# Gathers, combines, spline rows and a norm spread over more attention heads; other order of loads, stores and gating around the experts

## The chip, the cores and the metric

One core of one Trainium2 chip runs the whole kernel: TensorE (PE) for matmuls and transposes, VectorE (DVE), ScalarE (ACT), GpSimd (POOL) and SyncE (SP), which here issues DMAs only. The metric is the device time of one execution in microseconds (us), as the median of several runs. All data are 32-bit floats except where a bf16 or int32 tile is named.

## The reference, cut to what matters

Two transformer layers over `x` of 4 batches x 512 tokens x 256 features. Each layer is "modulated": six vectors per batch, worked out from a small input `c`, scale, shift and gate the branches.

```python
# layer 0
mod = (silu(L0_c) @ L0_wmod).reshape(4, 6, 1, 256)         # sa, ca, ga, sb, cb, gb
ga, gb = sign(ga) * max(|ga|, 0.25), sign(gb) * max(|gb|, 0.25)
h = layernorm(x) * (1 + ca) + sa
q, k, v = split(h @ W + b)                                  # norms and sum over the tokens
x = x + ga * (q / |q|) * sum(k / |k| * v)
h = layernorm(x) * (1 + cb) + sb
x = x + gb * moe(h)
# moe: 2048 tokens, 32 experts, 6 chosen per token, at most 48 tokens an expert (first come)
#   yb[e] = (silu(g) * u) @ w_down[e],  g, u = split(xb[e] @ w_gate_up[e])   # [48,256]x[256,352], [48,176]x[176,256]
#   out[t] = sum over the token's experts of 16 * prob * yb[slot]            # dropped where the expert is full
#   out   += (silu(gs) * us) @ ws_down,  gs, us = split(h @ ws_gate_up)      # the shared expert
# layer 1, with its own mod
h = layernorm(x) * (1 + ca) + sa
q, k, v = h @ w_q + b_q, h @ w_k + b_k, h @ w_v + b_v       # 16 heads of 128
x = x + ga * (softmax(causal(q @ k.T / sqrt(128))) @ v @ w_o + b_o)
h = layernorm(x) * (1 + cb) + sb
gate_w, up_w, down_w = three cubic splines over control points  # 1024 x 256 each
x = x + gb * ((silu(h @ gate_w.T) * (h @ up_w.T)) @ down_w.T)
```

## The kernel before

The work is written out in one Python function. A scheduler orders the instructions of DVE, ACT, POOL and SP by program order and by what it thinks will be ready; PE's order from the experts on is the one written (`manual_schedule`). `tc.issue_after(i)` keeps what stands inside it from being issued ahead of instruction `i`. Every engine works through its own list in order, so a waiting instruction holds all that stand behind it on its engine.

**Front, 0 to about 150 us.** Layer 0's attention and the routing of its experts, batch by batch. `choose` and `place` (L542, L615) find each token's experts and places; `place` makes four one-hot tiles `oh` per batch on DVE (L649), which PE reads (L654). The routed rows go to a table in HBM. SP loads the weights of the first `NEARLY` = 5 expert pairs while there is room (L472).

**Experts, about 150 to 240 us.** 32 experts in 16 pairs. `NLOAD` = 8 slots hold the weights of eight pairs, `wg` (704 KB) and `wd` (352 KB): pair q+8 is loaded when pair q has left its slot (`load_experts`, L454, called at L870). For each pair PE does `gate_up(q+1)`, `act_turned(q)`, `turned(q+2)` and `down(q-1)`, with a piece of the shared expert (`shared_down`) and of layer 1's modulation between them. `down(q)` ends in `ysb`, a tile with two buffers: ACT writes it from PSUM (L839); POOL scatters its rows for batch 0 into `planes` in HBM (L855; the last four pairs go by a one-hot matmul instead, `combined`); an ACT-queue DMA stores all of it into `ytab` in HBM (L868), from where batches 1 to 3 are gathered later. Hence `ysb(q+2)` can be written only when the store and the scatter of `ysb(q)` have landed. The PSUM tile `py` of `down` has one buffer, so `down(q+1)` needs `ysb(q)` written.

At q = 8, SP issues the loads of the biases `bia` (three of 8 KB) and `bo`, then of layer 1's first attention weights w_q, w_k, w_v (L957 to L963). ACT scales each w_q (`scale_q`, L758). At q = 12, `read_back` (L905) reads `planes` back as four tiles `yr`, after all scatters. `gated(i)` (L920) sums the six rows of a token, adds the shared expert `ysum[0]` (L928), multiplies by the gate (L929) and adds to `x` (L930); it runs on POOL for i = 0 and on DVE for i = 1 to 3. Then come the last pieces of the shared expert, copied from PSUM by ACT (L726), and layer 1's first norm.

**Attention of layer 1, about 246 to 996 us.** 64 heads (4 batches x 16), one loop step n each (L1504), of about 11.6 us. The projections (`project`, `values`) and the output product (`out_step`) are done by a seven-product scheme, for which POOL makes sums and differences of the weights (`weight_forms`, `out_weights`, `out_forms`); PE reads these early and late in a step. Beside it, in program order, run: `gather` (L278) of batches 1 to 3, six rounds r of four tiles i each, added into `ysum[b]` by DMAs that POOL prepares; `combine(b)` (L290), which gates the sum and adds it to `x` on DVE, all four tiles in the step with n mod 16 = 10; `norm(b)`, with its statistics (`ln_stats`, L186), one step later; `spline(u)` (L1118), 24 units of six DVE instructions and two PE transposes; `ffn_forms` on POOL; and at n = 59 in program order `ffn_norm(0)`, which is bound to no instruction.

**FFN of layer 1, about 996 to 1172 us.** Not touched.

DMAs issued by SP go into one hardware queue (q1 in the profile), those issued by ACT into another (q10), POOL's indirect ones into a third (q0). The scheduler gives SP's and ACT's DMAs eight semaphores in turn, so a DMA waits until the one eight before it, of either engine, has landed.

Of the kernel before, what the change touches and what calls it, by code (L numbers as in the profile page):

```python
# [34 lines left out]
NEARLY = 5  # L35
# [45 lines left out]
def kernel(ctx: ExitStack, tc: tile.TileContext, a: dict, out: bass.AP):  # L81
# [99 lines left out]
    last_pow = [None]  # L181
# [4 lines left out]
    def ln_stats(b, name, after):  # L186

        st = small.tile([P, NTT, 6], F32, tag="st", name=f"st_{name}{b}")
        ag = small.tile([P, NTT, 2], F32, tag="ag", name=f"ag_{name}{b}")
        with after_or_not(after):  # L190
            for i in range(NTT):
                nc.vector.bn_stats(st[:, i, :], xs[b][:, i, :])
                nc.vector.bn_aggr(ag[:, i, :], st[:, i, :])
        rs = small.tile([P, NTT], F32, tag="rs", name=f"rs_{name}{b}")
        nc.vector.tensor_scalar_add(rs, ag[:, :, 1], EPS)
        last_pow[0] = nc.gpsimd.tensor_tensor(rs, rs, nhalf, ALU.pow)
        return ag, rs
# [80 lines left out]
    def gather(b, r, after):  # L278

        for i in range(NTT):  # L280
            ga = nc.gpsimd.indirect_dma_start(  # L281
                out=ysum[b][:, i, :],
                out_offset=None,
                in_=ytab[:, :],
                in_offset=bass.IndirectOffsetOnAxis(ap=code[:, b * NTT + i, r : r + 1], axis=0),
                compute_op=ALU.add,
            )
            wait_for(ga, [after])

    def combine(b, after):  # L290

        for i in range(NTT):
            y, xi = ysum[b][:, i, :], xs[b][:, i, :]
            with tc.issue_after(after.ins):
                nc.vector.tensor_tensor(y, y, gbr[:, b, :], ALU.mult)
                nc.vector.tensor_tensor(xi, xi, y, ALU.add)
# [5 lines left out]
    with ExitStack() as l0:  # L302
# [312 lines left out]
        def place(b):  # L615
# [32 lines left out]
            for i in range(NTT):  # L648
                oh = rp.tile([P, CAP, E], BF16, tag="oh", name=f"oh{b}{i}", bufs=3)  # L649
                nc.vector.tensor_tensor(  # L650
                    oh, posb[:, i : i + 1, :].to_broadcast([P, CAP, E]), iota_c, ALU.is_equal
                )
                for q in range(4):
                    nc.tensor.matmul(  # L654
                        pix[32 * q : 32 * q + 32, :, :],
                        lhsT=tok[:, b * NTT + i, :],
                        rhs=oh[:, :, 8 * q : 8 * q + 8],
                        start=(i == 0),
                        stop=(i == NTT - 1),
                    )  # L660
# [54 lines left out]
        def shared_down(i):  # L715

            pd = psa.tile([P, D], F32, tag=f"su{i % 2 if i < NEXP or i >= NI - 4 else 0}", name=f"pd{i}", bufs=1)
            for c, n in enumerate(SHC):
                nc.tensor.matmul(
                    pd,  # L720
                    lhsT=sT[0:n, c, i * P : (i + 1) * P],
                    rhs=wsd[0:n, c, :],
                    start=(c == 0),
                    stop=(c == 2),
                )
            nc.scalar.copy(ysum[i // NTT][:, i % NTT, :], pd)  # L726
# [46 lines left out]
        ewp.append(ew.enter_context(tc.tile_pool(name="ew2", bufs=1)))  # L773
        for q in range(NEARLY, NLOAD):
            loaded.append(load_experts(q))
        with tc.tile_pool(name="eps", bufs=2, space=PSUM) as ps:
# [43 lines left out]
            def down(q):  # L820
# [47 lines left out]
                nc.scalar.dma_start(out=ytab[1 + q * P : 1 + (q + 1) * P, :], in_=ysb)  # L868
                if q + NLOAD < NPAIR:
                    loaded.append(load_experts(q + NLOAD))  # L870
                if q + 8 < NPAIR:
                    fetched(q + 8)
# [47 lines left out]
            def gated(i, after):  # L920

                eng = nc.vector if i else nc.gpsimd
                yr, xi, h3 = back[i], xs[0][:, i, :], 3 * D
                with tc.issue_after(after.ins):
                    eng.tensor_tensor(yr[:, 0:h3], yr[:, 0:h3], yr[:, h3:], ALU.add)
                    for w in (1, 2):
                        eng.tensor_tensor(yr[:, 0:D], yr[:, 0:D], yr[:, w * D : (w + 1) * D], ALU.add)
                    eng.tensor_tensor(yr[:, 0:D], yr[:, 0:D], ysum[0][:, i, :], ALU.add)  # L928
                    eng.tensor_tensor(yr[:, 0:D], yr[:, 0:D], gbr[:, 0, :], ALU.mult)  # L929
                    eng.tensor_tensor(xi, xi, yr[:, 0:D], ALU.add)  # L930

            w1, s1 = load_mod_inputs(m1p, 1, nc.scalar)
            with tc.manual_schedule(engines={mybir.EngineType.PE}):
# [8 lines left out]
                for q in range(NPAIR + 1):  # L942
# [12 lines left out]
                    if q == NPAIR - NLOAD:  # L955
                        with tc.issue_after(last_load[0].ins):
                            for j, n in enumerate(("b_q", "b_k", "b_v")):  # L957
                                nc.sync.dma_start(out=bia[:, j, :], in_=a[n])
                            nc.sync.dma_start(out=bo, in_=a["b_o"])
                            load_qk(0)  # L960
                            load_v(0)
                            for n in (1, 2):
                                load_qk(n)  # L963
                    if q == NPAIR - NDIR:
                        read_back()
                    if q in (3, 5, 7):
# [18 lines left out]
                for i in range(NI - 4, NI):  # L985
                    shared_down(i)
# [5 lines left out]
        for j in range(3):  # L992
            nc.sync.dma_start(out=win[:, j, :, :], in_=a["windows"][j].rearrange("(r p) k -> p r k", p=P))
# [112 lines left out]
    with ExitStack() as att1:  # L1106
# [11 lines left out]
        def spline(u):  # L1118
            r, j = divmod(u, 3)
            t, c = basis[r], win[:, j, r, :]  # L1120
            w = sp.tile([P, D], F32, tag="spw", name=f"spw{u}")
            nc.vector.tensor_scalar_mul(w, t[:, 1, :], c[:, 1:2])
            for q in (2, 3, 4):
                nc.vector.scalar_tensor_tensor(w, t[:, q, :], c[:, q : q + 1], w, ALU.mult, ALU.add)  # L1124
# [27 lines left out]
        def norm(b):  # L1152
            hT = new_hT(hp, b, "a1")
            ln_transposed(np_, ps, "pj", 1, b, SA, CA, hT, "a1")
# [6 lines left out]
        def weight_forms(key, w, early):  # L1161
# [4 lines left out]
            if early:  # L1166
# [3 lines left out]
                nc.gpsimd.tensor_tensor(w2, A22, w3, ALU.subtract)  # L1170
                wc[key] = {2: w2, 3: w3}
            else:
# [324 lines left out]
        gathers = {r + 1: (1, r) for r in range(TOPK)}  # L1497
        for b in range(2, B):
            for r, n in enumerate((-4, -3, 2, 3, 4, 5)):
                gathers[(b - 1) * NH + n] = (b, r)  # L1500
# [3 lines left out]
        for n in range(NHD + 1):  # L1504
# [13 lines left out]
            project(n + 1, 2)  # L1518
            out_step(n, 1) if n >= LAG else free()
# [9 lines left out]
            with tc.issue_after(last_form[0].ins):  # L1529
                out_prepare(n)  # L1530
            load_qk(n + 4)
            if n == 1:
                load_v(2)
            elif n % 4 == 0 and n:
                load_v(n // 4 + 2)
            if n % 2 == 0 and 6 <= n and unit < 3 * NCH:
                with tc.issue_after(evicted[n].ins):
                    spline(unit)
                if unit in (1, 4, 7):
                    ffn_forms(unit // 3, early[:, unit // 3])  # L1540
# [18 lines left out]
            if n in gathers:  # L1559
                gather(*gathers[n], evicted[n])  # L1560
            if n // NH + 1 < B:
                if n % NH == 10:
                    combine(n // NH + 1, evicted[n])
# [3 lines left out]
            if n == NHD - 5:  # L1567
                ffn_norm(0)
# [229 lines left out]
```

## Time and profile before

| | |
|---|---|
| median of 3 runs | 1174.84 us (1174.59 to 1176.95) |
| the profiled execution | 1174.33 us |
| its span, first to last instruction | 1172.6 us |
| mean granted TensorE clock | 0.988 |
| PE busy | 1121.6 us, 96% |
| DVE / POOL / ACT busy | 860.2 / 621.2 / 536.3 us |
| HBM traffic | 73 GB/s over the span; 268 to 304 GB/s from 152 to 205 us |

An instruction in a timeline is given with its start, its duration, its engine and line, what it writes and reads, and in brackets how long its engine had stood idle before it and what ended the wait. `PEclk` is the clock that PE was granted. Line numbers are those of the kernel before.

### The profile page before, as it was taken

Reading aid. Unit: us, or ns where it says so; the run is one execution under the profiler, and the core shown is the slowest. Engines: PE = TensorE matmul, PEld = TensorE weight load, DVE = VectorE, ACT = ScalarE, POOL = GpSimd, SP = SyncE. Lnnn points to the kernel's source line nnn. Section 1 sums busy time; section 2 is a strip of 40 time slices with the busy share of each in tenths; the row PEclk is TensorE's granted clock in tenths of the full one; section 3 lists DMA queues with packets and bytes.
Section 4 is the critical chain, followed back from the end, with each engine's and each line's share of the span. In section 5 each row is a group of like instructions: output and inputs, shape, how many; then the busy total and the mean of one; then the engine's idle time right before and its main releaser. Section 6 shows DMA issues by size and latency. Waiting matters only on the chain.

```text
span 1172.6 us, 16886 instructions
## 1 busy us (share of the span) xinstructions
PE 1121.6 (96%) x5220; PEld 823.0 (70%) x5220; DVE 860.2 (73%) x2596; ACT 536.3 (46%) x1373; POOL 621.2 (53%) x945
## 2 busy tenths in 40 slices
PE   6888999879999999999999999999999999999998
PEld 2434354457777777777778777777777777888887
DVE  5688623467888788788887888888877677467765
ACT  3542223335555545554555555554555455333321
POOL 3354124328974856965565975444535655344331
PEclk9999899889999999999999999999999999999999
DMA  7801289734421312321221431011010000000001
GB/s 268 285 26 43 83 250 284 227 113 84 88 64 41 76 43 66 75 68 36 66 57 46 94 64 59 26 39 60 28 37 28 19 18 1 1 1 19 18 1 37
DMA packets 80486, 86.10 MB, mean 73 GB/s; under 512 B 12158, under 2 KB 64748, under 8 KB 80268
## 3 DMA queue, kind: packets, MB, share of 16 engines
q1 hardware_dynamic: 65564, 68.10, 18.6%
q0 software_dynamic: 11712, 13.25, 6.8%
q10 hardware_dynamic: 3120, 3.68, 1.0%
q8 instruction: 42, 0.69, 0.2%
q14 instruction: 48, 0.39, 0.1%
HBM read 73.84 MB, written 11.55 MB: 73 GB/s over the span
## 4 chain that ended last, share of the span: by engine, by line
PE 61%; DVE 9%; POOL 3%; ACT 3%; issue 1%; DMA 1%; SPq 0%; ACTq 0%; DVEq 0%; POOLq 0%
PE s L1293 10%; PE o L1334 9%; PE po L1029 7%; PE P0p L1029 6%; PE fP L1029 6%; PE pt L1325 5%; PE P1p L1029 4%; PE P2p L1029 3%; PE acc L1029 3%; PE P0v L1029 3%; PE P2v L1029 2%; PE P1v L1029 2%; POOL ysum L281 1%; DVE spw L1124 1%; DVE nm L1305 1%
## 5 line engine op out<-in xcount | busy, mean ns | idle before, releaser
L1308 ACT ACTIVATE p<-s,nm 128x512 f32<-128x512 f32 (+3 forms) x256 | 135.4, 529 | 117.1 <-DVE nm L1305 115.0
L1293 PE MATMUL s<-qk,qk 128*128 128x512 f32 (+3 forms) x512 | 170.2, 435 | 1.3 <-DVE qk L1201 1.0
L1334 PE MATMUL o<-pT,v 128*128 128x512 f32 (+3 forms) x512 | 148.6, 433 | 0.2 <-DVE u3v L1213 0.2
L1334 PEld LDWEIGHTS o<-pT,v 128*128 128x128 f32 x512 | 96.8, 190 | 55.0 <-issue 30.6
L1327 ACT COPY pT<-pt 128x512 f32<-128x512 f32 (+1 forms) x192 | 98.4, 513 | 68.2 <-PE pt L1325 66.4
L1305 DVE TENSOR_REDUCE nm<-s 128x1 f32<-128x512 f32 (+3 forms) x256 | 124.1, 485 | 4.0
L281 POOL DMA_INDIRECT ysum<-ytab,code x72 | 113.0, 1570 | 20.4 <-issue 15.5
L1310 DVE TENSOR_SCALAR p<-p,den 128x512 f32<-128x512 f32 (+3 forms) x256 | 117.6, 460 | 3.4
L1325 PEld LDWEIGHTS pt<-ident,p 128*128 128x128 f32 x640 | 81.7, 141 | 34.4 <-issue 10.5
L1325 PE MATMUL pt<-ident,p 128*128 128x128 f32 x640 | 101.7, 273 | 0.3 <-DVE p L1310 0.3
L1303 DVE TENSOR_TENSOR s<-s,mask 128x128 f32<-128x128 f32 x256 | 73.5, 287 | 31.2 <-PE s L1293 31.2
L1168 POOL TENSOR_TENSOR w_p<-w_q,w_k 128x128 f32<-128x128 f32 x63 | 38.7, 615 | 87.2 <-ACT t1p L1207 53.0
L1293 PEld LDWEIGHTS s<-qk,qk 128*128 128x128 f32 x512 | 77.5, 191 | 5.9 <-issue 1.5
L1029 PE MATMUL P0p<-hT_a,w_q 128*128 128x256 f32 x252 | 75.0, 379 | 0.0
L1176 POOL TENSOR_TENSOR w_p<-w_k 128x128 f32<-128x128 f32 x63 | 29.9, 475 | 81.0 <-PE P2p L1029 81.0
L1029 PEld LDWEIGHTS P0p<-hT_a,w_q 128*128 128x128 f32 x252 | 47.5, 190 | 33.1 <-issue 29.9
L1309 DVE RECIPROCAL den<-den 128x1 f32<-128x1 f32 x256 | 40.4, 158 | 38.4 <-ACT p L1308 33.6
L1029 PE MATMUL P1p<-fT,w_p 128*128 128x256 f32 x252 | 64.9, 380 | 2.4 <-POOL w_p L1170 1.2
L1345 ACT ACTIVATE oH<-o,bia 128x512 f32<-128x512 f32 x64 | 44.0, 687 | 42.1 <-PE o L1334 41.1
L1201 DVE SCALAR_TENSOR_TENSOR qk<-P0p,bia,u3p 128x256 f32<-128x256 f32 x63 | 30.4, 482 | 37.1 <-ACT qk L1222 36.1
L1037 POOL TENSOR_TENSOR fI<-it 128x256 f32<-128x256 f32 x30 | 21.8, 728 | 67.0 <-DVE it L1623 67.0
L1029 PEld LDWEIGHTS P1p<-fT,w_p 128*128 128x128 f32 x252 | 47.6, 190 | 9.9 <-issue 1.9
(338 smaller groups left out, 2683.2 us busy)
## 6 DMA issues: line engine op xcount, KB each, us to landing
wg<-in_w_gate_up SPq DMA_DIRECT2D x16, 704.0 KB
w_q<-in_w_q SPq DMA_DIRECT2D x64, 128.0 KB
w_k<-in_w_k SPq DMA_DIRECT2D x64, 128.0 KB
w_v<-in_w_v SPq DMA_DIRECT2D x16, 512.0 KB
wd<-in_w_down SPq DMA_DIRECT2D x16, 352.0 KB
basis<-in_basis SPq DMA_DIRECT2D x8, 640.0 KB
planes<-zero SPq DMA_DIRECT2D x4, 768.0 KB
yr<-planes SPq DMA_DIRECT2D x4, 768.0 KB
```

The lines of the kernel that those rows point to most:

```text
L281: ga = nc.gpsimd.indirect_dma_start(out=ysum[b][:, i, :], out_offset=None, in_=ytab[:, :], in_offset=bass.IndirectOffsetOnAxis(ap=code[:, ...
L1029: nc.tensor.matmul(out, lhsT=lhsT, rhs=rhs, start=start, stop=stop, skip_group_check=shared)
L1293: nc.tensor.matmul(s[:, at[i] : c], lhsT=qk[n, 0][:, i * P : (i + 1) * P], rhs=qk[n, 1][:, : (i + 1) * P], start=True, stop=True,)
L1303: nc.vector.tensor_tensor(s[:, e - P : e], s[:, e - P : e], mask, ALU.add)
L1305: nc.vector.tensor_reduce(nm, s[:, e - w : e], AX.X, ALU.max, negate=True)
L1308: nc.scalar.activation(p, s[:, e - w : e], AF.Exp, bias=nm, accum_out=den)
L1309: nc.vector.reciprocal(den, den)
L1310: nc.vector.tensor_scalar_mul(p, p, den)
L1325: nc.tensor.transpose(pt[:, c : c + P], probs[n, i][:, j * P : (j + 1) * P], ident)
L1327: nc.scalar.copy(pT, pt[:, :w])
L1334: nc.tensor.matmul(o[:, j * P :], lhsT=vs[n // 4][:, j, hc : hc + HD], rhs=pTs[n, j], start=(j == 0), stop=(j == NTT - 1),)
L1345: nc.scalar.activation(oT, o, AF.Identity, bias=bia[:, 2, h : h + 1])
```

## The change

The parts of the diff, in the order of the code:

- `NEARLY` 5 to 6: one pair more is loaded in the front, one less beside the experts; to make room, `oh` has two buffers instead of three.
- The loads of `bia` and `bo` stand ahead of the loads of pairs 6 and 7, and no longer at q = 8.
- The store of `ysb` into `ytab` is issued by SP, after the load of pair q+8, and no longer by ACT.
- `gated` no longer adds `ysum[0]`; a new `shared_gated(i)` gates it and adds it to `x` on DVE at q = 4 to 7.
- ACT's part of layer 1's first norm is issued after the last copy of the shared expert.
- `gather` handles one tile of one round at a time; 24 of them per batch are spread over 9 steps (batch 1, from n = 0) or 12 steps (from n = 12 and n = 28), up to three a step, six for one tile i before the next tile begins. The old form waited for `evicted[n]`; the new one is ordered by `issue_after` behind a weight form.
- `combine` handles one tile in each of four steps, and takes that tile's norm statistics with it; `ln_stats` uses them.
- `spline` is cut in two: three DVE instructions at odd n, three and the transposes at even n. `ffn_forms` of the first three chunks moves to n = 10, 26 and 42.
- `ffn_norm(0)` is bound to `evicted[59]`.
- The small `windows` loads stand in step 0 of the loop instead of ahead of the attention.

```diff
-NEARLY = 5
+NEARLY = 6
...
+        if b in stats:
+            _, ag = stats.pop(b)
+        else:
...
-    def gather(b, r, after):
-        for i in range(NTT):
-            ga = nc.gpsimd.indirect_dma_start(
...
-            wait_for(ga, [after])
-    def combine(b, after):
-        for i in range(NTT):
+    def gather(b, i, r):
+        nc.gpsimd.indirect_dma_start(
...
+    def combine(b, i, after):
...
+            nc.vector.tensor_tensor(xi, xi, y, ALU.add)
+            nc.vector.bn_stats(st[:, i, :], xi)
+            nc.vector.bn_aggr(ag[:, i, :], st[:, i, :])
...
-                oh = rp.tile([P, CAP, E], BF16, tag="oh", name=f"oh{b}{i}", bufs=3)
+                oh = rp.tile([P, CAP, E], BF16, tag="oh", name=f"oh{b}{i}", bufs=2)
...
+        for j, n in enumerate(("b_q", "b_k", "b_v")):
+            nc.sync.dma_start(out=bia[:, j, :], in_=a[n])
+        nc.sync.dma_start(out=bo, in_=a["b_o"])
         for q in range(NEARLY, NLOAD):
             loaded.append(load_experts(q))
...
-                nc.scalar.dma_start(out=ytab[1 + q * P : 1 + (q + 1) * P, :], in_=ysb)
                 if q + NLOAD < NPAIR:
                     loaded.append(load_experts(q + NLOAD))
+                nc.sync.dma_start(out=ytab[1 + q * P : 1 + (q + 1) * P, :], in_=ysb)
...
-                    eng.tensor_tensor(yr[:, 0:D], yr[:, 0:D], ysum[0][:, i, :], ALU.add)
...
+            def shared_gated(i, after):
+                y, xi = ysum[0][:, i, :], xs[0][:, i, :]
+                with tc.issue_after(after.ins):
+                    nc.vector.tensor_tensor(y, y, gbr[:, 0, :], ALU.mult)
+                    nc.vector.tensor_tensor(xi, xi, y, ALU.add)
...
+                    if 4 <= q < 8:
+                        shared_gated(q - 4, turned_back[q])
...
-            ln_transposed(np_, ps, "pj", 1, b, SA, CA, hT, "a1")
+            ln_transposed(np_, ps, "pj", 1, b, SA, CA, hT, "a1", None, None, last_down if b == 0 else None)
...
-        gathers = {r + 1: (1, r) for r in range(TOPK)}
-        for b in range(2, B):
-            for r, n in enumerate((-4, -3, 2, 3, 4, 5)):
-                gathers[(b - 1) * NH + n] = (b, r)
+        gathers, combined_at = {}, {}
+        for b in range(1, B):
+            todo, first_step = [(b, i, r) for i in range(NTT) for r in range(TOPK)], (0, 12, 28)[b - 1]
+            for n, m in enumerate((3, 3, 3, 3, 3, 3, 2, 2, 2) if b == 1 else (3, 3, 1, 1, 1, 1, 3, 3, 3, 3, 1, 1)):
+                gathers[first_step + n] = [todo.pop(0) for _ in range(m)]
+            for i, n in enumerate((3, 5, 7, 10) if b == 1 else (3, 8, 10, 13)):
+                combined_at[first_step + n] = b, i
...
+            gather_some(n, 1)
             out_step(n, 1) if n >= LAG else free()
...
+            gather_some(n, 3)
             load_qk(n + 4)
...
+            if n % 2 and 5 <= n and unit < 3 * NCH:
+                with tc.issue_after(evicted[n].ins):
+                    spline(unit, 0)
+            if n in (10, 26, 42):
+                with tc.issue_after(last_form[0].ins):
+                    ffn_forms(n // 16, early[:, n // 16])
...
-                    spline(unit)
-                if unit in (1, 4, 7):
-                    ffn_forms(unit // 3, early[:, unit // 3])
+                    spline(unit, 1)
...
-            if n in gathers:
-                gather(*gathers[n], evicted[n])
+            if n in combined_at:
+                combine(*combined_at[n], evicted[n])
...
-                if n % NH == 10:
-                    combine(n // NH + 1, evicted[n])
...
-                ffn_norm(0)
+                ffn_norm(0, evicted[n])
```

## The prediction

> **What bounds the kernel now.** First the page: busy shares in 40 slices of 29.3 us, and the granted clock.
>
> ```profile
> PE   6888999879999999999999999999999999999998
> ...
> PEclk9999899889999999999999999999999999999999
> ```
>
> PE is the bound at 96%; room is left only in the front and in slices 5 to 8. Then busy time by stretch (length, then busy us and instructions of PE, PEld, DVE, ACT, POOL, then clock, DMA share, GB/s):
>
> ```profile
> 118.46:121.88 3.42, 1.49 (x14) 0.31 (x13) 3.42 (x8) 3.27 (x4) 0.00 (x0) 1.00 0.75 235
> 121.88:128.70 6.82, 6.38 (x15) 2.42 (x11) 3.87 (x15) 0.29 (x2) 0.00 (x0) 0.50 0.29 114
> ...
> 165.00:185.00 20.00, 20.00 (x130) 12.04 (x130) 8.19 (x39) 8.14 (x20) 8.91 (x9) 1.00 0.97 304
> ...
> 210.62:217.45 6.83, 6.16 (x24) 2.93 (x26) 4.17 (x22) 2.89 (x8) 2.37 (x4) 0.50 0.98 229
> ...
> 244.76:251.58 6.82, 5.44 (x12) 3.09 (x13) 3.03 (x7) 1.99 (x5) 3.30 (x6) 0.50 0.00 1
> 246.07:996.00 749.93, 741.36 (x3499) 575.00 (x3500) 599.11 (x1779) 398.05 (x1076) 467.32 (x718) 1.00 0.21 51
> ```
>
> Attention has 8.6 us of PE idle in 750, so spreading its side work can win a few us at most. Beside the experts PE is full while DMA is at 97%. Two stretches run at half clock, each behind a pause. What those pauses waited for is in PE's waits from 200 to 255 us (us in total, times, longest):
>
> ```profile
> PE lt_a L226 <- ACT ysum L726: 5.0, 1, 5.0
> PE gu L802 <- DVE xT L795: 3.6, 1, 3.6
> PE y L825 <- ACT ysb L839: 0.6, 1, 0.6
> ```
>
> and from 255 to 1000 us:
>
> ```profile
> PE P2v L1029 <- DVE v L1200: 2.3, 3, 1.9
> PE P2p L1029 <- POOL oWTrue L1361: 1.2, 2, 0.7
> PE P1p L1029 <- POOL w_p L1170: 1.2, 1, 1.2
> ```
>
> Last, the timelines of SP, ACT and PE follow the `gu` wait back:
>
> ```profile
> 201.02 0.45 SPq L958 DMA_DIRECT2D bia<-in_b_k  x1
> ```
> ```profile
> 192.54 0.33 ACTq L868 DMA_DIRECT2D ytab<-ysb  x1
> ...
> 200.43 0.95 ACT L839 ACTIVATE ysb<-y,xg 64x256 f32<-64x256 f32 x2 [2.96 <-DMA ytab<-ysb]
> ...
> 209.76 0.36 ACTq L868 DMA_DIRECT2D ytab<-ysb  x1
> 210.22 0.32 ACT L810 ACTIVATE act<-gu 128x176 f32<-128x176 f32 x1 [4.81 <-DMA bia<-in_b_k]
> ```
> ```profile
> 211.29 2.62 PE L802 MATMUL gu<-wg,xT 128*64 128x352 f32 x8 [3.56 <-DVE xT L795]
> ```
>
> The 8 KB load of `b_k` stood behind expert weights on SP's queue for 8.7 us. ACT's next `ytab` store shared its semaphore, so ACT stood 4.81 us; `act` was queued behind the store, DVE's `xT` behind `act`, and PE's `gu` behind `xT`.
>
> **The change, part by part**, against the profiled execution's 1174.33 us (its span of 1172.6 and 1.7 around it).
>
> *Biases earlier: -6.6.* They are now issued among the front's loads, so this wait cannot come. It gives back PE's 3.56 us and, with the pause gone, half of the 6.16 us that PE was busy at clock 0.50: 3.1.
>
> *Store on SP, one pair less to load: +4.8.* The cover that ACT's own queue gave is lost: `ytab(q)` now stands behind the weights of pair q+8, and `ysb(q+2)` waits for it. On ACT's queue the buffer was free 7.9 us after the issue (192.54 to 200.43); a tiny load on SP's queue took 8.7. At the end, w_q, w_k, w_v (1.28 MB, 4.3 us at some 300 GB/s) stand ahead of `ytab(8)`, and ACT, in its list, has w_q scaling and `act(13)` ahead of `ysb(10)`. By bytes: before, the last expert weights landed at 208.7 (counted from SP's packets); one pair less is -3.6, a start later behind the biases +1.6, the w's +4.3: 211.0. With up to 2 us of landing, `ytab(8)` is through at about 212.6, `ysb(10)` is written by 213.6, and `down(11)` starts at about 214.2. It started at 216.6 before and would at 210.0 with the stall alone gone: +4.2, and I add 0.6 for `act(12)`, now behind the w_q too. Ends: 0 (PE never gets there early) and +11, the store loop of the rivals.
>
> Here a rule weighs against the change: the Trainium skill ("DMA: Bandwidth & Descriptors", Queues, rings and completion order) has each DMA engine alternate between SP's and ACT's rows, while one row is consumed in order. So a store on ACT's row takes turns with the weights, and on SP's row it waits for all of them: about 1 MB or 3.6 us more per store, 11.5 in place of 7.9, which would cost the +11. The rows: 8.7 us for the tiny loads on the weights' own queue against 7.9 on ACT's, a difference of 0.8 with a pair more outstanding than after. I follow the rows, and leave the rule to the range.
>
> *Shared expert out of `gated`: -2.2.* The three L928 on DVE go (0.83, 0.42 and 0.43 us at 231.74, 235.47 and 238.14), all on the chain from the `planes` reads to `lt_a` at 246.07: -1.7. ACT's last `ysum` copies (0.35 each) now precede its two `xn` (0.60), one of which stood between them: -0.5. The eight DVE operations of `shared_gated` (0.42 each, 3.4) fall in q = 4 to 7, where DVE is busy 8.19 of 20 us: nothing, unless one is ahead of an `xT` (0.4 each). The pause ahead of `lt_a` shrinks from 5.0 to about 3, and the half clock behind it stays. The second rule bears on this: "no PE-idle gaps >~3.4µs" (the Trainium skill, "TensorE: Matmul & The Clock Gate", HAM oscillation). By it a pause of 3 us keeps the clock, half of 5.44 us is saved (-2.7), and the sum would be 1165.1. But at 118.46, 1.93 us idle in 3.42 were enough for 0.50 behind it. I keep the half clock.
>
> *Front: +0.4.* `oh` with two buffers makes DVE's third and fourth one-hot of a batch wait for PE's `pix`, 0.2 to 1 us where PE is behind; ends 0 and +2 (a half-clock stretch moved).
>
> *Attention: -2.9.* Gathers: 72 before and after, 1.57 us each on POOL, but four in a row hold it 7.5 us with the gaps, and `w_p` came 1.2 us late behind such a row: -1.2. `oWTrue`, late twice: half of 1.2, -0.6. `P2v <- v` 1.9: DVE had `xn_f` of `ffn_norm(0)` (1.39 us at 775.16, and its chain) ahead of `v`; bound to step 59 it stands beside lighter DVE work: -1.9. `combine` one tile a step, spline in halves and the statistics move the same 0.42 to 0.74 us instructions without adding any: nothing, where DVE has 599 of 750 us. The windows' loads move on SP's queue behind `ytab(8)` and are wanted steps later: nothing. Against this, +0.8: gathers of one tile depend on each other, landing 3.8 us after their start, and single gathers now stand ahead of weight forms at every step, so some form comes late. Ends -5 (most idle goes) and +3 (0.1 us in 30 steps).
>
> Sum: -6.6 + 4.8 - 2.2 + 0.4 - 2.9 = -6.5: 1167.8 for such an execution, and 0.5 more for the median (1174.84 against 1174.33): 1168.3, put at 1168.5.
>
> **The rivals.**
> *Slower: the store loop.* With two `ysb`, two pairs take one store's time plus writing. A pair took about 5.0 us, two 10.0, of which 1.8 is writing, issue and scatter: so a store up to 8.2 us costs nothing, each us above costs 0.5 a pair, 4 over the eight pairs q = 4 to 11. It eats the whole gain at 9.8 us and makes the kernel slower by over 0.2% from 10.4; at 11 it is 1179.5. For it: the queue's order, and weights that took 8.2 to 12.3 us from issue to landing. Against it: with fewer bytes in the same stretch the backlog should be smaller.
> *Expert part gives nothing.* The stall comes back as a wait of `ysb` on `ytab(8)` behind the w's, +3 worse than I have it, and the pause before `lt_a` grows as the `planes` reads come later: 1173. For it: SP's order; against: half of `down`'s delay must come in one place.
> *Spreading gives nothing.* The chained gathers hold POOL for 1.9 us each, weight forms and out weights come late as often as before: attention 0 in place of -2.9, 1171.4. For: POOL is busy 22.3 of 25 us where it gathers. Against: the chain is only within a tile.
> *More.* Both half clocks vanish and the gathers hide: -2.7 and -2 more, 1163.8.
>
> **How the numbers follow.** Main 0.44 (1165.5 to 1171.5); spreading gives nothing 0.16; expert part gives nothing 0.13; store loop 0.16 (1177 to 1183); more 0.11. The range, 1163 to 1176.5, leaves out most of the store loop and a tail of "more". Under 0.2% (2.35 us) a measurement can hardly tell from no change: faster is below 1172.5, the main case, "more", most of "spreading" and a bit of "expert part": 0.66; same 0.16; slower, the loop with a little of the rest, 0.18.
>
> **What would show it.** Biases: no wait of `act` on `bia`, no clock of 0.50 near 210. Store: the wait of `ysb` on `ytab` is under 3 us at each q and longest at `ysb(10)`; if it is 1 us or more longer at every q from 4, the loop has come. `gated`: `lt_a` waits some 3 us, and starts near 242 after the -1.8 and -2.2. Attention: `P2v <- v` and `P1p <- w_p` fall under 0.7, PE idle there about 5.7. Front: `pix <- oh` grows by under 1 us. I am wrong if stores on SP land after more than 10 us, or if POOL is late for a form in most steps.

## The result, and the profile after

The changed kernel takes 1192.82 us (median of 4 executions, 1188.50 to 1196.66) beside 1175.88 for the kernel before: a ratio of 1.0157, 95% interval 1.0137 to 1.0178. By the ratio it is 18.5 us slower than the kernel before (these medians differ by 16.9); 1168.5 was predicted. The profiled execution has a span of 1189.2 us, the one before 1172.6. Cut at the first `lt_a` of layer 1's norm and at the last score product `s`, the difference lies in one part:

| part of the span, us | before | after | predicted |
|---|---|---|---|
| front and experts, to the first `lt_a` | 246.1 | 242.2 | -3.6 |
| attention, to the last `s` | 746.7 | 767.2 | -2.9 |
| rest | 179.8 | 179.8 | 0 |

So the sum for the front came out (-3.9), and the attention went the other way: +20.5. The front's figure is in part luck: 1.3 us of it lie ahead of the experts' first product `gu` (154.64 us in place of 155.96), where a stretch at half clock near 122 us lasted 3.4 us in place of 6.8, which was not forecast. Among the ten kept traces of kernels with this front, the changed kernel's among them, that `gu` starts anywhere from 152.8 to 159.2 us. From it to `lt_a` the kernel before takes 90.1 us, the changed one 87.5, the ten 83.8 to 88.1. Of the attention's +20.5, 14.2 are idle time of PE (22.4 in place of 8.2); the other 6.3 stand in the records as longer PE work, whose ends are modelled. Line numbers below are those of the kernel named; in the changed kernel `gather` is L283, `combine` L299 to L302, the forms of w_p (POOL's sums and differences of the weights) L1186 to L1195. SPq is the DMA queue of SP.

First the page of the changed kernel (busy tenths and clock by slice), then its busy time by stretch, with the columns of the prediction's rows.

```profile
PE   6888998989799999999999999999999999999998
...
PEclk9999999989999999999999999999999999999999
```
```profile
197.30:200.70 3.40, 3.40 (x9) 0.78 (x9) 0.00 (x0) 1.03 (x2) 2.70 (x3) 0.51 0.87 297
234.80:241.60 6.80, 4.31 (x20) 3.41 (x19) 5.50 (x17) 1.58 (x5) 1.95 (x3) 1.00 0.79 265
241.60:248.40 6.80, 6.21 (x13) 3.28 (x14) 3.34 (x7) 2.04 (x4) 3.61 (x7) 0.50 0.08 32
246.00:1010.00 764.00, 741.58 (x3480) 569.47 (x3479) 623.65 (x1770) 393.54 (x1070) 470.14 (x713) 1.00 0.21 50
282.00:310.50 28.50, 24.50 (x105) 16.31 (x104) 18.69 (x57) 13.02 (x37) 17.86 (x23) 1.00 0.32 66
310.50:341.00 30.50, 23.16 (x104) 16.18 (x102) 22.93 (x62) 13.05 (x37) 20.84 (x26) 1.00 0.30 52
```

PE's eleventh slice (297 to 327 us) has fallen from 9 to 7. Between 282 and 341 us PE is busy 47.7 of 59.0 us: about steps 3 to 7; the first batch's 24 gathers are spread over steps 0 to 8. Matched matmul by matmul with the execution before, PE runs 2.6 us ahead at 287 us and 12 us late at 364, and then loses only some 4 more. The clock is whole there; the half-clock stretches are where the prediction left one (behind the transition, with `lt_a` waiting 3.1 us) and near 197, not 210.

PE's waits in the experts and the transition (us in total, times, longest), then the largest in the attention:

```profile
PE y L834 <- ACT ysb L848: 6.3, 4, 2.8
PE lt_a L229 <- DMA basis<-in_basis: 3.1, 1, 3.1
```
```profile
PE pt L1344 <- DVE p L1329: 7.5, 6, 2.6
PE o L1353 <- DVE u3v L1232: 3.4, 3, 2.1
PE pt L1344 <- ACT pT L1346: 3.1, 5, 0.9
PE P2p L1041 <- POOL w_p L1193: 1.3, 1, 1.3
```

The 3.1 us of `lt_a` are put down to a load of `basis`, which `lt_a` does not read; in e2, which has the same front, the same wait is 2.7 us and is put down to ACT's `xn_a`. In the attention PE names DVE and ACT, hardly POOL. The waits of POOL in the attention, and its timeline of gathers, name the source:

```profile
POOL ysum L283 <- DMA ysum<-ytab,code: 59.2, 32, 3.1
```
```profile
267.27 1.54 POOL L283 DMA_INDIRECT ysum<-ytab,code  x1 [2.80 <-DMA ysum<-ytab,code]
271.80 1.56 POOL L283 DMA_INDIRECT ysum<-ytab,code  x1 [1.96 <-DMA ysum<-ytab,code]
276.43 1.55 POOL L283 DMA_INDIRECT ysum<-ytab,code  x1 [1.90 <-DMA ysum<-ytab,code]
```

and in the kernel before, four tiles of one round:

```profile
287.25 1.60 POOL L281 DMA_INDIRECT ysum<-ytab,code  x1
289.16 1.56 POOL L281 DMA_INDIRECT ysum<-ytab,code  x1 [0.30 <-issue]
291.02 1.63 POOL L281 DMA_INDIRECT ysum<-ytab,code  x1 [0.30 <-issue]
```

A gather adds into the tile that the gather before it adds into, so it starts when that one has landed: 4.5 to 4.6 us from start to start in these rows, where the four tiles of the kernel before followed each other in 1.9. Where the next tile begins, as at 283.74, the changed kernel's POOL does not wait either. Three in a step are 13.8 us, and a step is 11.6. The sum fits the delay: the first 18 gathers of the batch stand in six steps, 69.6 us, and from the first (254.72) to the nineteenth (336.88) 82.2 us pass, 12.6 more. The loss reaches PE by a long way round. SP's waits from 280 to 370 us, then the timelines of POOL, SP, ACT and DVE:

```profile
SPq L751 <- POOL w_p L1193: 16.2, 6, 5.3
```
```profile
303.14 1.56 POOL L283 DMA_INDIRECT ysum<-ytab,code  x1 [0.52 <-DMA ysum<-ytab,code]
304.14 1.04 POOL L1380 TENSOR_TENSOR oWTrue<-wo,oWTrue 128x128 f32<-128x128 f32 x1
304.55 1.04 POOL L1193 TENSOR_TENSOR w_p<-w_q,w_p 128x128 f32<-128x128 f32 x1
```
```profile
305.62 0.37 SPq L751 DMA_DIRECT2D w_q<-in_w_q  x1
```
```profile
308.33 0.42 ACT L767 ACTIVATE w_q<-w_q 128x256 f32<-128x256 f32 x1 [5.33 <-DMA w_q<-in_w_q]
308.91 0.58 ACT L1327 ACTIVATE p<-s,nm 128x384 f32<-128x384 f32 x1
```
```profile
309.62 0.16 DVE L1328 RECIPROCAL den<-den 128x1 f32<-128x1 f32 x1 [2.75 <-ACT p L1327]
312.43 1.49 DVE L299 TENSOR_TENSOR ysum<-ysum,gbr 128x256 f32<-128x256 f32 x1 [1.53 <-DMA ysum<-ytab,code]
```

The form `w_p` of L1193 stands behind a gather on POOL and is the last reader of a slot of w_q; so SP loads the next w_q late, at 305.62, when the form has ended (16.2 us of such waits, 0.9 in the same stretch before), ACT stands 5.33 us at scaling it, the exponentials `p` are behind that on ACT, `den` and `p` on DVE behind those, and PE's transposes `pt` last. Each engine's list passes the delay on to the next.

### The profile page after: what moved, and what is told of

It reads as the page before. It is cut to its first block, busy times and chain, and to the rows that moved or that the text cites. A ratio compares the mean times of both kernels' runs of the same rounds, so it can differ in the third digit from the quotient of the medians.

```text
span 1189.2 us, 16898 instructions
## 1 busy us (share of the span) xinstructions
PE 1125.8 (95%) x5220; PEld 819.8 (69%) x5220; DVE 889.2 (75%) x2601; ACT 534.4 (45%) x1373; POOL 627.0 (53%) x944
## 4 chain that ended last, share of the span: by engine, by line
PE 44%; DVE 6%; ACT 2%; issue 1%; POOL 1%; DMA 0%; ACTq 0%; DVEq 0%; POOLq 0%
PE o L1353 6%; PE s L1312 6%; PE fP L1041 6%; PE po L1041 5%; PE P0p L1041 4%; PE pt L1344 3%; PE acc L1041 3%; PE P1p L1041 3%; PE P2p L1041 3%; PE P0v L1041 2%; PE P2v L1041 1%; PE P1v L1041 1%; DVE p L1329 1%; DVE nm L1324 1%; DVE spw L1139 0%
## 5 line engine op out<-in xcount | busy, mean ns | idle before, releaser
L283 POOL DMA_INDIRECT ysum<-ytab,code x72 | 114.8, 1594 | 79.1 <-DMA ysum<-ytab,code 59.2
L1329 DVE TENSOR_SCALAR p<-p,den 128x512 f32<-128x512 f32 (+3 forms) x256 | 132.7, 518 | 2.6
L1186 POOL TENSOR_TENSOR w_p<-w_q,w_k 128x128 f32<-128x128 f32 x63 | 42.1, 669 | 68.3 <-ACT t1p L1226 37.0
L1195 POOL TENSOR_TENSOR w_p<-w_k 128x128 f32<-128x128 f32 x63 | 39.1, 621 | 61.0 <-PE P2p L1041 61.0
L1041 PEld LDWEIGHTS P1p<-fT,w_p 128*128 128x128 f32 x252 | 47.7, 190 | 7.4 <-POOL oF L1395 0.5
```

The source lines that it names most:

```text
L283: nc.gpsimd.indirect_dma_start(out=ysum[b][:, i, :], out_offset=None, in_=ytab[:, :], in_offset=bass.IndirectOffsetOnAxis(ap=code[:, b * N ...
L1041: nc.tensor.matmul(out, lhsT=lhsT, rhs=rhs, start=start, stop=stop, skip_group_check=shared)
L1186: nc.gpsimd.tensor_tensor(w3, A11, A21, ALU.subtract)
L1329: nc.vector.tensor_scalar_mul(p, p, den)
```

## The experiments

The kernel before was run beside each call; its medians there were 1173.96 to 1176.93. "Attention" is its length in the kernel's one profiled execution, cut as above. Executions of one kernel lie about 1% apart (e10: 1165.99 to 1177.86), so the ratio with its interval is read, and differences in us are worked out from it. How steady an attention is, the table shows: e2, e10 and e16 have the same one and take 739.5 to 740.2 us; the kernel before, e3, e9, e13, e14 and e15 share the old one and take 745.1 to 750.3. So a few us between two single attentions are a finding only where the ratios' intervals are apart as well.

| kernel | median, us | ratio to before, 95% | attention, us |
|---|---|---|---|
| changed kernel | 1192.82 | 1.0157 (1.0137 to 1.0178) | 767.2 |
| e1 gathers round by round | 1173.71 | 0.9989 (0.9975 to 1.0003) | 751.2 |
| e2 gathers and combine as before | 1161.62 | 0.9905 (0.9876 to 0.9934) | 739.5 |
| e3 front and experts only | 1171.37 | 0.9975 (0.9957 to 0.9992) | 746.4 |
| e4 before, gathers tile by tile | 1256.37 | 1.0702 (1.0662 to 1.0743) | 828.8 |
| e5 late combine | 1195.95 | 1.0180 (1.0152 to 1.0208) | 770.7 |
| e6 e1, gathers at the step's end | 1168.59 | 0.9950 (0.9936 to 0.9964) | 745.2 |
| e7 e2, whole spline | 1168.11 | 0.9956 (0.9942 to 0.9969) | 744.0 |
| e8 e2, norm unbound | 1164.24 | 0.9924 (0.9897 to 0.9951) | 740.5 |
| e9 before, biases early | 1175.15 | 1.0000 (0.9985 to 1.0015) | 745.1 |
| e10 e2, store on ACT | 1169.90 | 0.9970 (0.9957 to 0.9983) | 740.2 |
| e11 e5, gathers in pairs | 1175.46 | 1.0008 (0.9993 to 1.0023) | 751.4 |
| e12 e2, gathers among the forms | 1166.67 | 0.9927 (0.9907 to 0.9947) | 743.1 |
| e13 before, store on SP | 1180.68 | 1.0029 (1.0014 to 1.0044) | 748.1 |
| e14 e13, biases early | 1182.28 | 1.0040 (1.0023 to 1.0056) | 750.3 |
| e15 before, six early pairs | 1170.15 | 0.9965 (0.9946 to 0.9984) | 745.7 |
| e16 e2, five early pairs | 1170.23 | 0.9963 (0.9942 to 0.9983) | 739.9 |

### Which half of the change: e3 and e2

e3 is the kernel before with the changed front and experts; its attention (gathers, combine, spline, forms, `ffn_norm`) is the old one.

> The kernel before with the front and expert parts of the change alone: six early pairs, two oh buffers, biases early, store of ysb on SP, shared_gated, ACT's part of the norm behind the last copy. By the prediction's sum -6.6 + 4.8 - 2.2 + 0.4 = -3.6: 1171 to 1172.5; in the trace of the changed kernel the first product after the transition starts 3.7 us earlier, which says the same. If the attention[...] gives it back: 1175.

Measured 1171.37, a gain of 0.25% (2.9 us; the interval is 0.9 to 5.1), its attention unchanged at 746.4 us. The front's sum holds.

e2 is the changed kernel with the old gathers and all four combines in one step:

```diff
-    def gather(b, i, r):
+    def gather(b, r, after):
+        for i in range(NTT):
...
+            wait_for(ga, [after])
...
-            if n in combined_at:
-                combine(*combined_at[n], evicted[n])
+            if n in gathers:
+                gather(*gathers[n], evicted[n])
...
+                if n % NH == 10:
+                    for i in range(NTT):
+                        combine(n // NH + 1, i, evicted[n])
```

> The changed kernel with the gathers as before the change (four tiles of one round at a time, behind the last instruction of a step) and all four combines in one step again; expert part, split spline, forms, bound ffn_norm and the norm's statistics in combine as changed. Theory A (chain of gathers): 1167 to 1172, PE idle in the attention 6 to 8 us. Theory C (the split spline, moved forms and bound norm cost as well): 1176 or more.

Measured 1161.62, better than expected: 0.95% or 11.2 us faster than the kernel before. Its attention takes 739.5 us, and PE waits for next to nothing there. Rows of PE's waits from 246 to 1010 us, the largest first:

```profile
PE s L1314 <- DVE qk L1222: 0.6, 1, 0.6
PE P0v L1043 <- DVE v L1221: 0.5, 1, 0.5
PE P2v L1043 <- DVE v L1221: 0.4, 2, 0.2
PE pt L1346 <- DVE p L1331: 0.3, 1, 0.3
...
PE o L1355 <- DVE u3v L1234: 0.2, 1, 0.2
```

So all of the loss, and more, is in how gathers and combines were spread: 27.7 us of attention (767.2 less 739.5). e2 is the fastest kernel of the study.

### The chain of gathers: e1, e4, e5, e11

e1 keeps the number of gathers of each step and turns their order:

```diff
-            todo, first_step = [(b, i, r) for i in range(NTT) for r in range(TOPK)], (0, 12, 28)[b - 1]
+            todo, first_step = [(b, i, r) for r in range(TOPK) for i in range(NTT)], (0, 12, 28)[b - 1]
...
-            for i, n in enumerate((3, 5, 7, 10) if b == 1 else (3, 8, 10, 13)):
+            for i, n in enumerate((9, 9, 10, 10) if b == 1 else (12, 12, 13, 13)):
```

> The changed kernel with its 72 gathers in the same places and the same number a step, but taken round by round (tiles 0, 1, 2, 3 in turn) in place of tile by tile, so that two gathers into the same tile are four apart; combine, which now finds its tiles complete only with the last round, stands at the ninth and tenth step (two tiles each). Theory A (each gather waits for the landing of the one before it into the same tile, 4.6 us from one to the next, three a step are 13.8 us of a step of 11.6; POOL's weight forms come late behind them): POOL's wait on ysum falls from 59 us to under 10, PE's idle time in the attention from some 22 us to under 10, and the time to 1170 to 1175. Theory B (gathers spread among the weight forms cost, in whatever order, since they push the forms into DVE's operations from SBUF to SBUF): the time stays above 1184.

Measured 1173.71: 19.7 us of the changed kernel's time are gone (1.0157 less 0.9989), and with them every wait of POOL for a landing. PE's idle time in the attention is 11.6 us, a little over the 10 expected. e4 does the reverse to the kernel before, one thing only:

```diff
-        for i in range(NTT):
+        for j in range(NTT):
+            i, k = divmod(NTT * r + j, TOPK)
...
-                in_offset=bass.IndirectOffsetOnAxis(ap=code[:, b * NTT + i, r : r + 1], axis=0),
+                in_offset=bass.IndirectOffsetOnAxis(ap=code[:, b * NTT + i, k : k + 1], axis=0),
```

> The kernel before with one thing changed: its gathers, still four at a time behind the last instruction of the same steps, run through one tile's six rounds before the next tile's, as in the changed kernel; combine is at the tenth step either way. Theory A (a gather waits until the one before it into the same tile has landed, 4.6 us from start to start): four are 18 us in place of 7.5, in 18 steps, six of them in a row at the start; what POOL had free in those steps is about 4 us, so each costs several us: 1210 or more, with POOL's waits on ysum at 100 us or more. If the landing were hidden by the waits that POOL has anyway: 1175 to 1180.

Measured 1256.37, 7.0% slower. The waits of POOL and PE in its attention:

```profile
POOL ysum L282 <- DMA ysum<-ytab,code: 99.4, 42, 5.0
```
```profile
PE P2p L1030 <- POOL w_p L1177: 20.6, 6, 5.1
PE P1p L1030 <- POOL w_p L1171: 19.4, 8, 6.5
```

POOL waits 99.4 us for landings, and here PE stands at the forms themselves. The order of the gathers alone does it. e5 asks whether it was `combine`, which stood on DVE 4.8 us for gathers in the changed kernel; it keeps the gathers and has e1's steps for combine:

> The changed kernel with tile-by-tile gathers as they are, but combine of a batch only at the ninth and tenth step (batch 1) or the thirteenth and fourteenth (two tiles each), so that DVE no longer stands at a combine whose last gather has not landed. Theory A1 (POOL's chain alone sets it: weight forms late, so slots of w_q free late, loads late, ACT's scaling of w_q waits, and with it the exponentials): 1185 to 1190. Theory A2 (DVE's waits of 1.5 to 1.7 us at combine, at the head of its queue, are the larger part): 1174 to 1180.

Measured 1195.95 and an attention of 770.7: nothing gained. DVE's waits at combine are a symptom, and theory A2 falls. e11 is e5 with two tiles in turn:

```diff
-            todo, first_step = [(b, i, r) for i in range(NTT) for r in range(TOPK)], (0, 12, 28)[b - 1]
+            todo, first_step = [(b, i + k, r) for i in (0, 2) for r in range(TOPK) for k in range(2)], (0, 12, 28)[b - 1]
```

> e5 (gathers tile by tile, combine late) with the gathers of two tiles in turn, so that two into the same tile are two apart; e5 has them one apart, e1 four. The attention's length is 770.7 us in e5's trace and 751.2 in e1's. Theory A: three a step in pairs need about 7 to 8 us of a step of 11.6, POOL waits for a landing some 1 us where they stand close and not at all where forms lie between: attention 752 to 757, time 1174 to 1180, POOL's waits on ysum 5 to 20 us.

Measured 1175.46, attention 751.4, the same as with four in turn (751.2), and no wait for a landing at all, less than I expected. Where the next gather into a tile is the first, the second or the fourth behind the last one, the attention takes 770.7, 751.4 and 751.2 us: the chain costs 19.3 us, and one other gather between is enough.

### What is left of the spreading: e6, e12

e1 is still 11.7 us of attention behind e2. e6 takes e1's gathers from among the forms to the end of their step; the first batch's also begin one step later, and its four combines stand in one step:

```diff
+        wait_for(ga, [after])
...
-            gather_some(n, 1)
...
-            gather_some(n, 3)
...
+            for g in gathers.get(n, ()):
+                gather(*g, evicted[n])
```

> The kernel with gathers round by round (e1) once more, still two or three a step, but each behind the last instruction of its step as before the change, and not among the weight forms; the first batch's begin one step later, its four combines stand in one step. Theory B (what is left of e1's loss against e2, 12 us, comes from gathers standing ahead of weight forms, which then run beside DVE's spline and combine operations and slow both down): 1160 to 1165, as e2. Theory D (it is the spreading: more steps that hold a gather at all, or combine's place): 1170 or more.

Measured 1168.59, attention 745.2, between the two theories: the place, with the two smaller changes, is worth 6.0 us, and 5.7 are left that the spreading or the place of combine cost. e12 is the other corner, e2's four of a round put among the forms:

```diff
-            if n in gathers:
-                gather(*gathers[n], evicted[n])
...
+            gather_some(n, 1)
...
+            gather_some(n, 3)
```

> e2 with its four gathers of a round in the same steps, but issued as in the changed kernel, one ahead of the out product's forms and three behind them, not behind the step's last instruction. e2's attention is 739.5 us, e1's (spread and among the forms) 751.2, e6's (spread, behind the last instruction) 745.2. If the place among the forms costs by itself: attention 745 to 752, time 1167 to 1174. If it costs only together with the spreading: 739 to 741, 1161 to 1163.

Measured 1166.67, attention 743.1: 3.6 us for the place in this one execution, less than the 5.5 to 12.5 of the first theory and more than the second's. The intervals of e12 and e2 overlap, so that the place costs by itself is likely and not shown. What goes with such a place is to be seen in e1's timelines of DVE and POOL:

```profile
345.79 2.81 DVE L1139 SCALAR_TENSOR_TENSOR spw<-basis,win,spw 128x256 f32<-128x256 f32 x1
```
```profile
344.45 1.74 POOL L283 DMA_INDIRECT ysum<-ytab,code  x1
345.63 1.32 POOL L1394 TENSOR_TENSOR oH<-oH 128x256 f32<-128x256 f32 x1
346.41 1.21 POOL L1193 TENSOR_TENSOR w_v<-w_v,w_v 128x256 f32<-128x256 f32 x1
```

Behind a gather POOL has its forms in one run, and a spline operation of DVE beside that run takes 2.81 us in place of 0.5 to 0.9. The longest spline operation is 1.45 us in e12 and 0.95 in e2 and e6, whose gathers stand at the end of the step. The Trainium skill ("SBUF — State Buffer", SBUF: two separate sides) has a port pair that DVE and POOL lock in turn for a whole instruction; that fits, but 2.81 us are longer than any one of these POOL operations, and no run here takes the one engine's work away, so the cause is argued, and how 11.7 us divide among place, number of steps and combine is not settled.

### The split spline and the bound norm: e7, e8

e7 (the spline function in one piece again, and its call):

```diff
-                    spline(unit, 1)
+                    spline(unit)
+                if unit in (1, 4, 7):
+                    ffn_forms(unit // 3, early[:, unit // 3])
```

> e2 with the spline's six DVE instructions in one step again and the first three chunks' forms where they were. e2's attention is 7.2 us shorter than the one of the kernel before. If the split spline gives most of it (many waits of PE under 1 us, each behind DVE): 1166 to 1168. If the split gives nothing, as the prediction had it: 1161 to 1163.

Measured 1168.11, attention 744.0 in place of 739.5: the split spline with the moved forms gives 4.5 us, and the two intervals do not meet. PE's idle time there is 5.9 us, in e2 2.5, and the largest waits that e2 lacks are two:

```profile
PE P1p L1043 <- POOL w_p L1184: 1.3, 1, 1.3
PE P1p L1043 <- DVE x L251: 1.1, 2, 0.5
```

So the wait for `w_p`, which the prediction priced at the gathers, goes with the split spline and the moved forms, while four gathers still stand in a row. e8:

```diff
-                ffn_norm(0, evicted[n])
+                ffn_norm(0)
```

> e2 with ffn_norm(0) bound to no instruction again. By the prediction's term (1.9 us of PE waiting for v behind xn_f): 1163 to 1164, and the wait of P2v on v near 778 is back at 1.9. If the split spline has made room for it: 1161 to 1162.

Measured 1164.24, with an interval that reaches e2's time; the attention is 1.0 us longer, hardly more than equal attentions differ, and the wait of `P2v` on `v` is 0.4, not 1.9. Beside the split spline the norm is hardly in the way; one wait of 0.7 us on `oWTrue` is back. In e7, with the norm bound and the spline whole, the wait on `v` is 0.6: either change is enough for it.

### The terms of the front: e9, e10, e13 to e16

e9 moves the four bias loads alone.

> The kernel before with only the biases' loads moved ahead of those of pairs 5 to 7. The prediction's term for it alone: -6.6 (3.56 us of PE's wait for xT and 3.1 of half clock behind it), so 1168 to 1169. If ACT's store then waits at the same place for something else on SP's queue (the loads of w_q share its semaphores), the stall moves and stays: 1173 to 1175.

Measured 1175.15, ratio 1.0000. The wait on the biases is gone, and the next load on SP's queue has taken its place. ACT's timeline, where 4.81 us went to `bia`:

```profile
210.84 0.32 ACT L813 ACTIVATE act<-gu 128x176 f32<-128x176 f32 x1 [0.74 <-PE gu L805]
216.32 0.42 ACT L761 ACTIVATE w_q<-w_q 128x256 f32<-128x256 f32 x1 [5.16 <-DMA w_q<-in_w_q]
```

e10 is e2 with the store back on ACT:

```diff
+                nc.scalar.dma_start(out=ytab[1 + q * P : 1 + (q + 1) * P, :], in_=ysb)
                 if q + NLOAD < NPAIR:
                     loaded.append(load_experts(q + NLOAD))
-                nc.sync.dma_start(out=ytab[1 + q * P : 1 + (q + 1) * P, :], in_=ysb)
```

> e2 with the store of ysb issued by ACT again, ahead of the load of pair q+8. The prediction's term for the store on SP: +4.8 of loss, so e10 would be faster than e2's 1161.6 by about that: 1156 to 1158. If SP's queue is no slower for the store than ACT's: 1161 to 1163.

Measured 1169.90, 7.6 us slower than e2 by the ratios, where the forecast was 4 to 6 faster. In ACT's timeline it stands at w_q still longer:

```profile
206.03 0.42 ACT L769 ACTIVATE w_q<-w_q 128x256 f32<-128x256 f32 x1 [8.67 <-DMA w_q<-in_w_q]
```

So I took the store's move for the gain. e13 makes that move alone:

```diff
-                nc.scalar.dma_start(out=ytab[1 + q * P : 1 + (q + 1) * P, :], in_=ysb)
                 if q + NLOAD < NPAIR:
                     loaded.append(load_experts(q + NLOAD))
+                nc.sync.dma_start(out=ytab[1 + q * P : 1 + (q + 1) * P, :], in_=ysb)
```

> The kernel before with only the store of ysb moved to SP, behind the load of pair q+8. The prediction's term: +4.8, so 1179 to 1180. What e9 and e10 suggest (ACT, once it issues no stores, no longer stands at a store that shares a semaphore with a load behind the expert weights on SP's queue; the move is the gain): 1168 to 1171.

Measured 1180.68, 3.4 us slower: alone the move costs, as predicted, but not where it was predicted. ACT's waits at `ysb`, before and in e13:

```profile
ACT ysb L839 <- DMA ytab<-ysb: 8.1, 4, 3.0
```
```profile
ACT ysb L839 <- DMA ytab<-ysb: 14.9, 5, 4.2
```

e13's five stand at `ysb(3)` to `ysb(8)`, all along the loop, and not at `ysb(10)`. From the issue of a store to the end of the wait for it 6.9 to 12.3 us pass, 9.3 in the mean of the five; before it was 7.5 to 7.9. e14 adds the early biases.

> The kernel before with the biases early and the store on SP. The prediction's terms together: -6.6 + 4.8, 1172 to 1173. If the store's move is the gain and the biases' is none: as e13. If the sixth early pair is needed too (less left for the queue that then carries the stores): as the kernel before, 1174 to 1175, with the rest of e3's gain of 3.6 from the pair and from the shared expert's adds.

Measured 1182.28, 4.7 us slower: as e13 within the intervals, though the case that said so took the store's move for the gain. The biases do not help this kernel either. That leaves the pair, which e15 adds to the kernel before, alone:

```diff
-NEARLY = 5
+NEARLY = 6
...
-                oh = rp.tile([P, CAP, E], BF16, tag="oh", name=f"oh{b}{i}", bufs=3)
+                oh = rp.tile([P, CAP, E], BF16, tag="oh", name=f"oh{b}{i}", bufs=2)
```

> The kernel before with six pairs of expert weights loaded in the front in place of five, and two oh buffers to make the room; biases and store as before. If the expert stage ends when its bytes are through (one pair is 1.056 MB, 3.6 us at 290 GB/s), the pair alone gives e3's gain or most of it: 1171 to 1174 beside a kernel before of 1175 to 1177. If the pair helps only together with the store on SP: no faster than before.

Measured 1170.15, 4.1 us faster: at least as much as e3's whole front (2.9), and the intervals overlap. e16 takes the pair from e2.

> e2 with five early pairs and three oh buffers again; biases, store on SP and the rest as in e2. e14 (biases and store alone) lost 4.7 us to the kernel before, e3 (with the pair and the shared expert's adds) gained 3.6. If the pair is what turns the loss into the gain: e2's time and 6 to 9 us, 1168 to 1171. If the shared expert's adds and the order of the norm's copies do most of it: 1162 to 1165.

Measured 1170.23: e2 without the pair is 6.8 us slower by the ratios. Its 1.056 MB come through in the front, where DMA has time: busy 0.44 from 4 to 150 us in the kernel before, 0.97 from 165 to 185. From the first `gu` to `lt_a` the traces say the same: 90.1 us before, 91.6 in e9, 92.0 in e13, 95.7 in e14, 86.7 in e15; 83.8 in e2, 93.1 in e10, 92.1 in e16. What is not settled is why the store on SP costs 3.4 us alone and is worth 7.6 in e2: the two were not tried with the pair and nothing else.

## Why the prediction was wrong

*The attention, step "-2.9": this failed.* Its term for the gathers, -1.2 with +0.8 against it, is where it fell. Against e2, which has everything else of the changed attention, the spread gathers and combines cost 27.7 us. The prediction had both factors, a landing 3.8 us behind the start and up to three gathers a step into one tile, and named the dependence; but it priced the dependence as "some form comes late", 0.1 us in 30 steps, in place of multiplying: 3 x 3.8 = 11.4 us, a whole step of 11.6 already, and 3 x 4.6 = 13.8 with the distance that was measured. That product would have shown that POOL sets the pace through the first batch. The upper end of +3 rested on no row. The chain measured 19.3 us (e5 against e1); the place among the forms is not clear of the noise by itself (3.6 in e12).

*The other terms of the attention.* "Nothing" for the split spline was wrong by 4.5 us of gain (e7). The -1.9 for the bound norm was right as a wait, but the split spline alone ends that wait too (e8). The -1.2 for `w_p` and -0.6 for `oWTrue` can't be read from the changed kernel; in e2 both waits are gone with the gathers still four in a row. `w_p`'s is back in e7, 0.7 us of `oWTrue`'s in e8, so the gathers did not decide them.

*The expert stage, -1.8: right in sum by luck, wrong in its parts.* The biases' -6.6 is 0 (e9): their stall is the place where the end of the weights' bytes was felt, and without it ACT stands at w_q. The store's +4.8 is +3.4 without the pair (e13), and the gain comes from the pair, -4.1 (e15), whose 3.6 us were inside the store's term. One term too good and one too bad made the right sum.

*The store and the rule on queue rows.* The term of +4.8 came from one late wait at `ysb(10)`; it is not there, neither in e13 nor in the changed kernel, whose waits on `ytab` are at `ysb(2)`, `ysb(5)` and `ysb(6)`:

```profile
ACT ysb L848 <- DMA ytab<-ysb: 12.0, 3, 4.6
```

So the sign "under 3 us at each q and longest at `ysb(10)`" failed, and one of the three stores took 10.7 us, over the 10 named as a sign of being wrong. That the size came near (3.4 in e13) was luck of another path: the 9.3 us of a store in e13 lie between the 8.7 of the row and the 11.5 of the rule, and the loop's own sum, 4 us for each us above 8.2, gives 4.4 for them.

*`gated`, -2.2, and the clock.* `lt_a` waits 3.1 us, against about 3 forecast, and starts at 242.17, where it was expected, with the luck of the front in it. The half clock behind it stayed (0.50 from 241.60), as the row of the trace had it and the rule of 3.4 us idle had not.

*Front, +0.4.* PE's wait of `pix` on `oh` is 3.0 us in both executions: 0.

*The rivals.* "Spreading gives nothing" had the right mechanism, chained gathers on POOL, and stopped at zero; its "only within a tile" is no relief when six gathers of one tile follow each other. The rival on the slow side, the store loop, came in part in e13 and e14 and did not make the changed kernel slow; the slow side was reached by another way that I had in hand as a gain. The loop's 11 us are counted in two ways in the prediction: as an end of the store's term, in place of 4.8, they give 1174.5, and on top of the main case 1179.5.

## What to carry to other kernels

When operations that wait for each other are spread over steps, multiply the start-to-start time of the chain by the number in a step, and compare with the step before asking what they hide; put another tile's operation between two of the same tile. A stall on a small load behind large ones can mark where the bytes end: here moving the small load moved the stall, and moving a pair's bytes to an idle stretch gained 4.1 us. A sum that comes out right does not show its terms; one run for each does.

## What the hardware did that I had not expected

- A gather that adds into a tile could follow the one before it into the same tile only 4.5 to 4.6 us after its start, though POOL is busy 1.56 us with it; into another tile 1.9 us (timelines of the changed kernel and of the one before). The Trainium skill ("DMA: Bandwidth & Descriptors", Rules for kernel authors) says why the wait must be there: an accumulating DMA reads and writes its destination with nothing held in between, so the earlier one's semaphore has to be waited for.
- One DVE operation on 128x256 took 2.81 us beside a run of POOL's forms (e1), in place of 0.5 to 0.9; with the gathers at the end of the step none was longer than 0.95 (e2, e6).
- A half-clock stretch ahead of the experts lasted 6.8 us in one execution and 3.4 in the other (near 122 us), with the same waits of PE on `oh`, 3.0 us in all.
